# Graph message passing with residual layer norm: picking 336 instead of 294 source tiles on TensorE

## The chip, the cores and the metric

The kernel runs on one core of one Trainium2 chip. The metric is the device time of one launch in microseconds (us): the median of several runs. Next to it stands one profiled execution, from which all durations and waits are read.

A core has five engines that matter here. TensorE multiplies matrices (in the profile PE for the products and PEld for loading the stationary operand). VectorE (DVE) and ScalarE (ACT) do elementwise work. GpSimd (POOL) issues the indirect DMAs, and SyncE (SP) issues the plain ones. Each engine works through its own list of instructions in order and waits where a semaphore says so.

## The reference, cut to what matters

There are 6250 nodes with 64 features and 200000 edges, sorted by destination. Cut to its core:

```
w    = silu(edge_attr_32 @ W1 + b1) @ W2 + b2          # 200000 x 9
msg  = einsum('ef,em,fmg->eg', x[src], edge_attr_9 * w, W_tp)
agg  = segment_sum(msg, dst, 6250) / sqrt(16)
gamma, beta = split(silu(node_vec[:, None] @ Wn1 + bn1) @ Wn2 + bn2)
out  = layernorm(x + agg * (1 + gamma) + beta)
```

The costly item for this change is `x[src]`: one row of 64 floats has to be fetched for each of 200000 edges.

## The kernel before

**Tiles and groups.** Edges are cut into 1563 tiles of 128 and the tiles into 98 groups of 16 (`NBLK`, `KB`; the last group has 11). The array `hs` of a group is filled with the source rows of its 16 tiles. It has seven buffers (`AHEAD + 1`), so gathers can be up to six groups ahead.

**Three ways to fetch rows.** (1) `gather(g)`, line 91: one indirect DMA by GpSimd for each tile. (2) `load_rows`, line 106: in 16 of the groups (`SPG`, every sixth from group 7) the first tile comes as 128 single-row DMAs that SyncE issues, 22 of them in each of the six loops before. (3) `pick(g, t)`, line 482: the last `Q` = 3 tiles of each group are fetched by TensorE from a copy of x that lies in SBUF. For this the source number is split in `setup` (lines 207 to 230) into a partition, a block h of 7 and a place of 7. The first two become keys, which are written to the DRAM array `kd` and come back with `load_keys`. `keys(g, j)` multiplies the key rows with ones, so that they stand on every partition of the PSUM tile `pk` (line 458), and compares them with the partition number into the one-hot matrix `hot_k` (line 464, one VectorE instruction for three tiles). `pick` then makes 14 products of 128x128 by 128x448 (7 blocks, the two halves of x in `xs`) into the PSUM tile `px`. VectorE masks the place with `scalar_tensor_tensor` (`xm`, line 491) and sums into the column of `hs` (line 493). `px` and `xm` have two buffers each.

**The loop.** The order of all engines' work is written out by hand (`tc.manual_schedule()`). Loop i, of 98, issues in this order:

- on GpSimd `gather(i+6)`; on SyncE, in even loops, `load(i+2)` (edge features `ea` and `sh` of two groups, lines 374 and 376), in odd ones `load_keys`, then the rows of `load_rows`
- `pick(i+1, 0)`; between its products TensorE makes those of `place(i-2)` (line 559, PSUM tile `pd`) and of `keys(i+2, i-2)`, which holds the product for the gate too (line 357, into the fourth quarter of `pk`)
- `hidden(i+2)` (line 405) with its silu on ScalarE (line 413), `second(i+1)` (line 422), which writes the PSUM tile `p2`
- `windows(i)` (line 511): 32 small products of `hs` of group i; it waits for the gathers of that group, and it frees the group's buffer of `hs`
- `pick(i+1, 1)`; between its products `weights(i+1)` (the transposes of line 432, which read ScalarE's `p2s`) and `project(i-1)` (line 537, PSUM tile `pr`)
- every fourth loop, from loop 6, `finish` (lines 622 to 639): the layer norm of two blocks of nodes on VectorE and ScalarE, and the output DMA on SyncE
- `pick(i+1, 2)`

**Shared PSUM banks.** A tag of the PSUM pool is one place that is handed on in order. `pk` and `pr` share tag "r"; `pd` and `p2` share tag "s"; `px` has two places. A writer waits until the previous tile's last reader is done.

Of the kernel before, what the change touches and what calls it, by code (L numbers as in the profile page):

```python
# [7 lines left out]
F32 = mybir.dt.float32  # L8
I32 = mybir.dt.int32
BF16 = mybir.dt.bfloat16  # L10
# [5 lines left out]
P = 128  # L16
N, F, M, D, H, E = 6250, 64, 9, 32, 64, 200000
NJ = 49
# [7 lines left out]
FB = 2  # L26
AHEAD = 6
LB = 2
Q = 3
J = 7  # L30
SPG = range(7, NBLK, 6)
SPR = 22
# [16 lines left out]

def picked(g):  # L50

    return Q


def tiles(g):
# [4 lines left out]
def gnn_resnorm_kernel(ctx: ExitStack, tc: tile.TileContext, x, src, dst, dst_row, ea, sh, cn,  # L60
# [18 lines left out]
    with ExitStack() as fast:  # L79
# [56 lines left out]
        def setup(temp):  # L136
# [84 lines left out]
            nc.vector.tensor_scalar(kh, ti[1], float(P), None, op0=ALU.mult)  # L221
            for c0 in range(0, C, P):
                n = min(P, C - c0)
                p_kt = psum.tile([P, 2, P], F32, tag=("s", "r", "s")[c0 // P], name=f"p_kt{c0}")
                for i, half in enumerate((kp, kh)):
                    nc.tensor.matmul(p_kt[0:n, i, :], half[:, c0:c0 + n], ident, start=True, stop=True)
                kt = temp.tile([P, 2, P], BF16, name=f"kt{c0}")
                nc.scalar.copy(kt[0:n], p_kt[0:n])
                nc.sync.dma_start(kd[:, c0:c0 + n, :].rearrange("i c e -> c i e"), kt[0:n])
            nc.vector.scalar_tensor_tensor(jl, kh, -float(J) / P, rest, op0=ALU.mult, op1=ALU.add)  # L230
# [35 lines left out]
            def between(h):  # L266

                if h == 0:
                    p_f = psum.tile([KB, NBLK], F32, tag="s", name="p_f")
                    nc.tensor.matmul(p_f, first_t, ident[0:NBLK, 0:NBLK], start=True, stop=True)  # L270
                    nc.scalar.copy(first_f, p_f)
                elif h == 1:
                    for f in keys(0, -1):
                        f()
                elif h == 3:
                    p_cn = psum.tile([P, NJ], F32, tag="s", name="p_cn")
                    nc.tensor.matmul(p_cn, cn_j, ident[0:NJ, 0:NJ], start=True, stop=True)
                    cn_s = temp.tile([P, NJ], F32)
                    nc.scalar.copy(cn_s, p_cn)
                    nc.sync.dma_start(cn_d, cn_s)  # L280
                    nc.sync.dma_start(wn1c, wn1.rearrange("o h -> h o"))
                    nc.sync.dma_start(bn1c, bn1.unsqueeze(1))
                    gate_load(0)
                    nc.sync.dma_start(wn2a[0:H, :], wn2)
                    nc.sync.dma_start(wn2a[H:H + 1, :], bn2.unsqueeze(0))
                    for q in range(2):
                        n = (M + 1 - q) // 2
                        nc.sync.dma_start(wtc2[q * F:(q + 1) * F, 0:n, :], wtp[:, q:M:2, :])
                    load(LB)
                    with nc.allow_non_contiguous_dma(reason="2048 words, once"):  # L290
                        nc.sync.dma_start(src_r, src[:, SPG[0] * KB:NBLK * KB:6 * KB].rearrange("p g -> g p"))
# [9 lines left out]
                    hidden_act(0)  # L301
                between(h)
            pick(0, 0)
            for f in keys(1, -1):
                f()
            base(0)
            near(0)
            second(0)
# [8 lines left out]
            ids()  # L317
            hidden(1)
            nc.scalar.copy(acc_r, zero.to_broadcast([P, NJ * F]))
            pick(0, 2)  # L320
            nc.sync.dma_start(xb, x.rearrange("(j p) f -> p j f", p=P))
            for s in range(2):
                nc.sync.dma_start(w2bd[s * H:(s + 1) * H, s, :], w2)
# [30 lines left out]
            nc.scalar.activation(ht[j0 // 4 % 2][0:H, :nj], cb.pop(j0)[:, :nj], AF.Silu, bias=bn1c, scale=wn1c)  # L354

        def gate(j, pe):
            nc.tensor.matmul(pe, ht[j // 4 % 2][:, j % 4], wn2a, start=True, stop=True)
            nc.vector.tensor_scalar(gam[:, j, :], pe[:, 0:F], 1.0, 0.25, op0=ALU.add, op1=ALU.mult)
            nc.vector.tensor_add(xb[:, j, :], xb[:, j, :], pe[:, F:2 * F])

# [87 lines left out]

        hot_k = {}

        def keys(g, j):

            pk = psum.tile([P, Q + 1, P], F32, tag="r", name=f"pk{g}")
            q = picked(g)

            def part(k):
                if k == 0:
                    nc.tensor.matmul(pk[:, 0:q, :].rearrange("p t e -> p (t e)"), ones2,  # L458
                                     kr_t.pop(g).rearrange("i t e -> i (t e)"), start=True, stop=True)
                else:  # L460
                    gate(j, pk[:, Q, :])
                if k == n - 1:
                    hot_k[g] = late.tile([P, Q, J, P], F32R, tag="hot_k", name=f"hot_k{g}")
                    nc.vector.tensor_tensor(hot_k[g][:, 0:q], pk[:, 0:q].unsqueeze(2).to_broadcast([P, q, J, P]),  # L464
                                            nk[:, None, :, None].to_broadcast([P, q, J, P]), op=ALU.is_equal)

            n = 2 if 0 <= j < NJ else 1
            return [lambda k=k: part(k) for k in range(n)]

        def pick(g, t, other=()):  # L470


            other = [f for fs in other for f in fs]
            q = picked(g) if g < NBLK else 0
            if t >= q:
                for f in other:
                    f()
                return
            px = psum.tile([P, F, J], F32, tag="px", name=f"px{g}_{t}", bufs=2)
            for h in range(J):  # L480
                for i in range(2):
                    nc.tensor.matmul(px.rearrange("p f l -> p (f l)"), hot_k[g][:, t, h, :],  # L482
                                     xs[i][:, h].rearrange("p f l -> p (f l)"),
                                     start=(h == 0 and i == 0), stop=(h == J - 1 and i == 1))
                    if i == 1 and other:
                        other.pop(0)()
            for f in other:
                f()
            xm = late.tile([P, F, J], F32, tag="xm", name=f"xm{g}_{t}")
            c = (g + 1) * Q - q + t  # L490
            nc.vector.scalar_tensor_tensor(xm, li[:, None, :].to_broadcast([P, F, J]), jl[:, c:c + 1], px,  # L491
                                           op0=ALU.is_equal, op1=ALU.mult)
            nc.vector.tensor_reduce(hs[g][:, tiles(g) - q + t, :], xm, AX.X, ALU.add)  # L493
# [54 lines left out]
        def place(g):  # L548

            if not 0 <= g < NBLK:  # L550
                return []
            kb = lo_block(g)
            js = [j for j in (0, 1) if 0 <= kb + j < NJ]
            pd = {}

            def part(j):
                if j == js[0]:
                    pd[g] = psum.tile([P, 2, F], F32, tag="s", name=f"pd{g}")
                nc.tensor.matmul(pd[g][:, j, :], hot[g][:, j * P:(j + 1) * P], r[g], start=True, stop=True)  # L559
                if j == js[-1]:  # L560
                    hot.pop(g), r.pop(g)
                    b0, b1_ = kb + js[0], kb + js[-1] + 1
                    nc.vector.tensor_add(acc[:, b0:b1_, :], acc[:, b0:b1_, :], pd[g][:, js[0]:js[-1] + 1, :])

            return [lambda j=j: part(j) for j in js]

        done = 0
        with tc.manual_schedule(), tc.tile_pool(name="temp", bufs=1) as temp:
            setup(temp)

            for i in range(NBLK):
                if i + AHEAD < NBLK:
                    gather(i + AHEAD)
                if i % LB == 0 and i + LB < NBLK:
                    if i > 0:
                        load(i + LB)
                    near(i + LB)
                if i % LB == 1 and i + 1 + LB < NBLK:
                    load_keys(i + 1 + LB)
                if i % 4 == 3 and i + 1 < NJ:  # L580
                    gate_load(i + 1)
                for g in SPG:
                    if 0 < g - i <= AHEAD:
                        load_rows(g, (AHEAD - g + i) * SPR)
                pick(i + 1, 0, [place(i - 2)] + ([keys(i + 2, i - 2)] if i + 2 < NBLK else []))
                if 3 <= i <= 5:
                    reach(i - 3)
                if i + 2 < NBLK:
                    hidden(i + 2)
                if i + 1 < NBLK:  # L590
                    second(i + 1)
                if i < NBLK - 2:
                    windows(i)
                if i % 4 == 1 and i - 1 < NJ:
                    gate_hidden(i - 1)
                if i + 1 < NBLK:
                    pick(i + 1, 1, [weights(i + 1), project(i - 1)])
                else:
                    for f in project(i - 1) + place(i - 1):
                        f()  # L600
                ready = max(lo_block(i if i == NBLK - 1 else i - 1), 0)
                while ready - done >= (FB if ready < NJ - 1 else 1):
                    finish(done, min(done + FB, ready))
                    done = min(done + FB, ready)
                pick(i + 1, 2)
                if i >= NBLK - 2:
                    windows(i)
                if i == NBLK - 2:
                    sums(i + 1)
# [204 lines left out]
```

## Time and profile before

| what | value |
|---|---|
| median of 3 runs | 1590.99 us (1590.33 to 1592.33) |
| the profiled execution, its own time | 1590.71 us |
| span of the profiled execution, first to last instruction | 1588.9 us |
| around the span | 1.8 us |
| busy: TensorE / GpSimd / VectorE / ScalarE | 89% / 75% / 62% / 30% |
| granted TensorE clock, mean | 0.961 |
| gathers by GpSimd / tiles picked | 1253 / 294 |

The busy share of an engine is that of its instructions' own time. GpSimd's 75% has to be read together with its gaps: between two gathers lie 0.3 us that the profile puts down to "issue", which means that the engine waited for nothing that the profile shows. A line of a timeline gives the start, the duration, the engine and source line, and in square brackets the idle time of the engine just before, with what ended it.

### The profile page before, as it was taken

Reading aid. Unit: us, or ns where it says so; the run is one execution under the profiler, and the core shown is the slowest. Engines: PE = TensorE matmul, PEld = TensorE weight load, DVE = VectorE, ACT = ScalarE, POOL = GpSimd, SP = SyncE. Lnnn points to the kernel's source line nnn. Section 1 sums busy time; section 2 is a strip of 40 time slices with the busy share of each in tenths; the row PEclk is TensorE's granted clock in tenths of the full one; section 3 lists DMA queues with packets and bytes.
Section 4 is the critical chain, followed back from the end, with each engine's and each line's share of the span. In section 5 each row is a group of like instructions: output and inputs, shape, how many; then the busy total and the mean of one; then the engine's idle time right before and its main releaser. Section 6 shows DMA issues by size and latency. Waiting matters only on the chain.

```text
span 1588.9 us, 33055 instructions
## 1 busy us (share of the span) xinstructions
PE 1407.5 (89%) x10206; PEld 1143.1 (72%) x10206; DVE 992.6 (62%) x1611; ACT 473.1 (30%) x1187; POOL 1186.0 (75%) x1262
## 2 busy tenths in 40 slices
PE   5999999988989888989898989888889899888886
PEld 3777778767777777777676767676777777776765
DVE  6676667665656565665665656656566666565664
ACT  4323223323232323232322323323223232322232
POOL 7777777777777777777777777777777777777773
PEclk9999999999999999999999999999999999999998
DMA  5312222221211121212111221121111211211110
GB/s 155 84 48 50 62 50 54 58 50 50 61 50 50 45 66 45 50 50 61 48 47 45 52 57 47 47 62 46 45 47 47 62 46 47 62 47 45 47 46 20
DMA packets 86199, 85.42 MB, mean 54 GB/s; under 512 B 37625, under 2 KB 52013, under 8 KB 86014
## 3 DMA queue, kind: packets, MB, share of 16 engines
q0 software_dynamic: 40096, 41.14, 11.7%
q1 hardware_dynamic: 45156, 40.44, 8.4%
q8 instruction: 83, 1.36, 0.4%
q10 hardware_dynamic: 762, 1.64, 0.3%
q14 instruction: 102, 0.84, 0.2%
HBM read 81.35 MB, written 1.78 MB: 52 GB/s over the span
## 4 chain that ended last, share of the span: by engine, by line
PE 33%; POOL 32%; issue 14%; DMA 10%; SPq 7%; DVE 2%; ACT 1%; POOLq 0%; ACTq 0%; DVEq 0%
POOL hs L91 32%; PE px L482 21%; DMA hs<-in_x_dram,src_i 9%; SPq L106 4%; PE pz L511 4%; PE pr L537 2%; PE p L405 2%; SPq L101 2%; PE p L422 1%; PE p L432 1%; PE pd L559 1%; DMA ea<-in_ea_dram 1%; DVE xm L491 0%; DVE hs L493 0%; PE pk L458 0%
## 5 line engine op out<-in xcount | busy, mean ns | idle before, releaser
L91 POOL DMA_INDIRECT hs<-in_x_dram,src_i x1253 | 1184.7, 945 | 382.6 <-issue 347.3
L482 PE MATMUL px<-xs,hot_k 128*128 128x448 f32 x4116 | 1100.4, 400 | 3.2 <-DVE xs L299 3.2
L482 PEld LDWEIGHTS px<-xs,hot_k 128*128 128x128 f32 x4116 | 717.9, 196 | 62.1 <-DVE xs L299 3.6
L491 DVE SCALAR_TENSOR_TENSOR xm<-li,jl,px 128x448 f32<-128x448 f32 x294 | 199.1, 677 | 213.0 <-PE px L482 211.2
L464 DVE TENSOR_TENSOR hot_k<-pk,nk 128x2688 fp32r<-128x2688 f32 x98 | 289.4, 2953 | 4.6 <-PE pk L458 4.6
L413 ACT ACTIVATE st<-p,b1c 128x1024 f32<-128x1024 f32 x98 | 109.1, 1114 | 560.1 <-PE p L405 559.9
L511 PE MATMUL pz<-a,hs 128*64 128x72 f32 x3126 | 135.0, 245 | 134.0 <-DMA hs<-in_x_dram,src_i 79.7
L521 ACT COPY zt<-pz 64x160 f32<-64x160 f32 (+2 forms) x784 | 213.4, 272 | 128.9 <-PE pz L511 110.8
L511 PEld LDWEIGHTS pz<-a,hs 128*64 128x64 f32 x3126 | 121.1, 151 | 177.5 <-issue 161.6
L438 DVE TENSOR_TENSOR p<-p,sh 128x72 f32<-128x72 f32 x196 | 47.3, 241 | 296.0 <-PE p L432 224.3
L537 PEld LDWEIGHTS pr<-wtc,zt 128*128 128x128 f32 x980 | 190.0, 196 | 20.8 <-ACT zt L521 5.2
L493 DVE TENSOR_REDUCE hs<-xm 128x64 f32<-128x448 f32 x294 | 182.3, 620 | 10.1
L537 PE MATMUL pr<-wtc,zt 128*128 128x64 f32 x980 | 165.0, 252 | 5.0 <-ACT zt L521 5.0
L444 DVE TENSOR_TENSOR a<-oh,p 128x1152 f32<-128x1152 f32 x98 | 132.6, 1354 | 3.3
L405 PE MATMUL p<-ea,w1bd 64*128 64x512 f32 x392 | 113.5, 657 | 5.6 <-DMA ea<-in_ea_dram 5.5
L542 ACT COPY r<-pr 128x64 f32<-128x64 f32 x98 | 20.8, 212 | 261.3 <-PE pr L537 261.3
L559 PEld LDWEIGHTS pd<-r,c 128*128 128x128 f32 x388 | 73.1, 190 | 7.3 <-ACT r L542 1.0
L422 PEld LDWEIGHTS p<-st,w2p 128*32 128x32 f32 x784 | 15.6, 109 | 74.3 <-issue 72.1
L559 PE MATMUL pd<-r,c 128*128 128x64 f32 x388 | 64.6, 249 | 0.7 <-ACT r L542 0.7
L422 PE MATMUL p<-st,w2p 128*32 128x256 f32 x784 | 63.5, 396 | 0.0
L432 PE MATMUL p<-ident,p2s 128*128 128x128 f32 x196 | 58.9, 301 | 3.9 <-ACT p2s L425 3.8
L413 ACT ACT_TABLE_LOAD x23 | 29.5, 1283 | 94.7 <-PE p L405 94.7
(103 smaller groups left out, 456.6 us busy)
## 6 DMA issues: line engine op xcount, KB each, us to landing
hs<-in_x_dram SPq DMA_DIRECT2D x2048, 0.2 KB
ea<-in_ea_dram SPq DMA_DIRECT2D x49, 512.0 KB
hs<-in_x_dram,src_i POOLq DMA_INDIRECT x1253
sh<-in_sh_dram SPq DMA_DIRECT2D x49, 144.0 KB
cb<-cn_d SPq DMA_DIRECT2D x12, 128.0 KB
out_dram<-o SPq DMA_DIRECT2D x24, 64.0 KB
gam<-in_x_dram ACTq DMA_DIRECT2D x2, 448.0 KB
dst_i<-in_dst_dram SPq DMA_DIRECT2D x1, 784.0 KB
```

Source lines behind the costliest of these rows:

```text
L91: hs_dma[g] = [nc.gpsimd.indirect_dma_start(out=hs[g][:, t - g * KB, :], out_offset=None, in_=x, in_offset=bass.IndirectOffsetOnAxis(ap=sr ...
L405: nc.tensor.matmul(p1[:, i, :], w1bd[i * 64:(i + 1) * 64, :], e[i * 64:(i + 1) * 64, :], start=True, stop=True)
L413: nc.scalar.activation(st[g], p1_t.pop(g), AF.Silu, bias=b1c)
L444: nc.vector.tensor_mul(a[g], oh_t.pop(g)[:, :, None, :].to_broadcast([P, KB, M, W]), sw.unsqueeze(3).to_broadcast([P, KB, M, W]))
L464: nc.vector.tensor_tensor(hot_k[g][:, 0:q], pk[:, 0:q].unsqueeze(2).to_broadcast([P, q, J, P]), nk[:, None, :, None].to_broadcast([P, q, J ...
L482: nc.tensor.matmul(px.rearrange("p f l -> p (f l)"), hot_k[g][:, t, h, :], xs[i][:, h].rearrange("p f l -> p (f l)"), start=(h == 0 and i ...
L491: nc.vector.scalar_tensor_tensor(xm, li[:, None, :].to_broadcast([P, F, J]), jl[:, c:c + 1], px, op0=ALU.is_equal, op1=ALU.mult)
L493: nc.vector.tensor_reduce(hs[g][:, tiles(g) - q + t, :], xm, AX.X, ALU.add)
L511: mm = nc.tensor.matmul(pz[v * F:(v + 1) * F, k // 2].rearrange("p m w -> p (m w)"), hsg[:, k0 + k, :], ag[:, k0 + k].rearrange("p m w -> ...
L521: nc.scalar.copy(z[h * F:(h + 1) * F, 0:5 - h, k0 + v:k0 + n:2, :].rearrange("p m k w -> p k m w"), pz[v * F:(v + 1) * F, 0:(n + 1 - v) // ...
L537: nc.tensor.matmul(pr[g], z[:, c].rearrange("p k w -> p (k w)"), wtc2[:, c, :], start=(c == 0), stop=(c == 4))
L559: nc.tensor.matmul(pd[g][:, j, :], hot[g][:, j * P:(j + 1) * P], r[g], start=True, stop=True)
```

## The change

`Q` becomes 4, and `picked(g)` returns 4 for groups whose number is 1, 3 or 5 modulo 7, and 3 for the others: 336 tiles are picked, 42 more, and 42 fewer are gathered. Two groups of four are never neighbours. The PSUM tile `pk` of 512 floats[...] holds up to four tiles of keys. The gate's product, which had the fourth quarter of it, moves to the second half of the `pd` tile and is issued as the first product of `place`, ahead of the two that it had followed. Its two VectorE instructions follow the addition to `acc`. The one-hots are made by one VectorE instruction for each tile, into seven buffers of one tile; two of them are issued inside `pick(i+1, 0)` and the rest behind its `xm` and sum. In `setup` the arrays of keys have 392 columns instead of 294, with four chunks through PSUM instead of three.

```diff
-Q = 3
+Q = 4
...
 def picked(g):
-    return Q
+    return Q - (4 * g % 7 < 4)
...
-                p_kt = psum.tile([P, 2, P], F32, tag=("s", "r", "s")[c0 // P], name=f"p_kt{c0}")
+                p_kt = psum.tile([P, 2, P], F32, tag=("s", "r")[c0 // P % 2], name=f"p_kt{c0}")
...
-                kt = temp.tile([P, 2, P], BF16, name=f"kt{c0}")
+                kt = acc_r[:, 6 * C + c0:6 * C + c0 + P].bitcast(BF16).rearrange("p (i e) -> p i e", i=2)
...
-            pick(0, 2)
+            for t in range(2, Q):
+                pick(0, t)
...
         def gate(j, pe):
-            nc.tensor.matmul(pe, ht[j // 4 % 2][:, j % 4], wn2a, start=True, stop=True)
...
+        pk_t = {}
+        def keys(g):
+            pk_t[g] = psum.tile([P, Q, P], F32, tag="r", name=f"pk{g}")
+            nc.tensor.matmul(pk_t[g][:, 0:picked(g), :].rearrange("p t e -> p (t e)"), ones2,
+                             kr_t.pop(g).rearrange("i t e -> i (t e)"), start=True, stop=True)
+        def hots(g, t0, t1):
+            for t in range(t0, min(t1, picked(g))):
+                hot_k[g, t] = late.tile([P, J, P], F32R, tag="hot_k", name=f"hot_k{g}_{t}", bufs=7)
+                nc.vector.tensor_tensor(hot_k[g, t], pk_t[g][:, t, None, :].to_broadcast([P, J, P]),
+                                        nk.unsqueeze(2).to_broadcast([P, J, P]), op=ALU.is_equal)
...
         def place(g):
-            pd = {}
+            pd = psum.tile([P, 4, F], F32, tag="s", name=f"pd{g}")
+            pe = pd[:, 2:4, :].rearrange("p a f -> p (a f)")
...
+                    if g < NJ:
+                        gate(g, pe)
+            parts = [lambda j=j: part(j) for j in js]
+            if g < NJ:
+                parts.insert(0, lambda: nc.tensor.matmul(pe, ht[g // 4 % 2][:, g % 4], wn2a, start=True, stop=True))
+            return parts
...
-                pick(i + 1, 0, [place(i - 2)] + ([keys(i + 2, i - 2)] if i + 2 < NBLK else []))
+                pick(i + 1, 0, [place(i - 2)] + ([[lambda: keys(i + 2), lambda: hots(i + 2, 0, 2)]]
+                                                 if i + 2 < NBLK else []))
+                if i + 2 < NBLK:
+                    hots(i + 2, 2, Q)
...
-                pick(i + 1, 2)
+                for t in range(2, Q):
+                    pick(i + 1, t)
```

More of the change, by code (lines that the diff above doesn't have):

```diff
@@ L272, in between @@
                 elif h == 1:
-                    for f in keys(0, -1):
-                        f()
+                    keys(0)
+                    hots(0, 0, Q)
                 elif h == 3:
@@ L303, in setup @@
             pick(0, 0)
-            for f in keys(1, -1):
-                f()
+            keys(1)
+            hots(1, 0, Q)
             base(0)
@@ L449, in gnn_resnorm_kernel @@
         hot_k = {}
[L451 to L468, printed above, removed]
+        pk_t = {}
[8 more added lines that the diff above has]
+                                        nk.unsqueeze(2).to_broadcast([P, J, P]), op=ALU.is_equal)
         def pick(g, t, other=()):
@@ L481, in pick @@
                 for i in range(2):
-                    nc.tensor.matmul(px.rearrange("p f l -> p (f l)"), hot_k[g][:, t, h, :],
+                    nc.tensor.matmul(px.rearrange("p f l -> p (f l)"), hot_k[g, t][:, h, :],
                                      xs[i][:, h].rearrange("p f l -> p (f l)"),
@@ L553, in place @@
             js = [j for j in (0, 1) if 0 <= kb + j < NJ]
-            pd = {}
+            pd = psum.tile([P, 4, F], F32, tag="s", name=f"pd{g}")
+            pe = pd[:, 2:4, :].rearrange("p a f -> p (a f)")
             def part(j):
-                if j == js[0]:
-                    pd[g] = psum.tile([P, 2, F], F32, tag="s", name=f"pd{g}")
-                nc.tensor.matmul(pd[g][:, j, :], hot[g][:, j * P:(j + 1) * P], r[g], start=True, stop=True)
+                nc.tensor.matmul(pd[:, j, :], hot[g][:, j * P:(j + 1) * P], r[g], start=True, stop=True)
                 if j == js[-1]:
@@ L562, in part @@
                     b0, b1_ = kb + js[0], kb + js[-1] + 1
-                    nc.vector.tensor_add(acc[:, b0:b1_, :], acc[:, b0:b1_, :], pd[g][:, js[0]:js[-1] + 1, :])
-            return [lambda j=j: part(j) for j in js]
+                    nc.vector.tensor_add(acc[:, b0:b1_, :], acc[:, b0:b1_, :], pd[:, js[0]:js[-1] + 1, :])
+                    if g < NJ:
[4 more added lines that the diff above has]
+            return parts
         done = 0
```

## The prediction

> **What bounds the kernel now.** I read the page first, then the waits of TensorE, the table of windows, and TensorE's timeline at two places.
>
> ```profile
> span 1588.9 us, 33055 instructions
> PE 1407.5 (89%) x10206; PEld 1143.1 (72%) x10206; DVE 992.6 (62%) x1611; ACT 473.1 (30%) x1187; POOL 1186.0 (75%) x1262
> ...
> L91 POOL DMA_INDIRECT hs<-in_x_dram,src_i x1253 | 1184.7, 945 | 382.6 <-issue 347.3
> L482 PE MATMUL px<-xs,hot_k 128*128 128x448 f32 x4116 | 1100.4, 400 | 3.2 <-DVE xs L299 3.2
> ...
> L491 DVE SCALAR_TENSOR_TENSOR xm<-li,jl,px 128x448 f32<-128x448 f32 x294 | 199.1, 677 | 213.0 <-PE px L482 211.2
> L464 DVE TENSOR_TENSOR hot_k<-pk,nk 128x2688 fp32r<-128x2688 f32 x98 | 289.4, 2953 | 4.6 <-PE pk L458 4.6
> ```
>
> POOL's 1184.7 busy and 382.6 idle us are its whole list: 1253 gathers, one each 1.249 us, from 2.8 to 1568.3 us, next to no true wait. POOL is full at "75%". TensorE's waits:
>
> ```profile
> PE pz L511 <- DMA hs<-in_x_dram,src_i: 79.7, 39, 3.5
> PE pz L511 <- issue: 42.2, 25, 2.9
> PE pz L511 <- DMA hs<-in_x_dram: 12.0, 8, 1.8
> ```
>
> Nearly all of TensorE's recorded idle time, 133.9 us, lies ahead of `windows`, which needs the group's gathers. The windows say since when:
>
> ```profile
> 200.00:300.00 100.00, 97.17 (x739) 79.10 (x738) 70.55 (x120) 33.65 (x85) 75.61 (x81) 1.00 0.20 52
> 1000.00:1100.00 100.00, 89.04 (x652) 72.64 (x648) 60.50 (x96) 30.65 (x79) 75.60 (x81) 0.95 0.19 49
> ```
>
> Until 310 us TensorE runs without waiting for rows (97%), then at POOL's pace (89%). The first stretch shows what a loop costs TensorE alone; the second, the wait:
>
> ```profile
> 238.71 1.22 PE L511 MATMUL pz<-a,hs 128*64 128x72 f32 x32
> ...
> 244.06 3.54 PE L482 MATMUL px<-xs,hot_k 128*128 128x448 f32 x16
> 247.45 0.33 PE L559 MATMUL pd<-r,c 128*128 128x64 f32 x2
> ...
> 252.46 0.35 PE L511 MATMUL pz<-a,hs 128*64 128x72 f32 x4
> ```
>
> ```profile
> 823.04 1.22 PE L511 MATMUL pz<-a,hs 128*64 128x72 f32 x32 [2.61 <-DMA hs<-in_x_dram,src_i]
> ```
>
> TensorE needs 13.75 us (252.46 - 238.71) for a loop; POOL 13 x 1.249 = 16.24 us, or 14.99 in the 16 groups with a tile from SyncE. A pick is 14 products at 3.39/16 us (from the two middle lines): 2.95 us.
>
> **What the Trainium skill says.** "VectorE: DVE Perf Modes", The TRN2 errata, gives fp32 tensor_tensor (N+151)/0.96 ns. For N = 2688 that is 2957; the trace has 2953. So I use it for the one-hots of one tile, which no row shows: N = 896, 1091 ns (an estimate). "Perfetto Trace Analysis", DMA Instruction — SWDGE (GPSIMD): the end in the profile is that of writing descriptors, not of the data. The trace agrees: in the bound stretch `windows` starts about 2.6 us after its last gather starts, though that lasts 0.94. "TensorE: Matmul & The Clock Gate", What's actually happening: an idle window of about 3.4 us halves the clock. Here 2.75 us did: the 32 products at 839.38, after that wait, took 2.19 us instead of 1.22. With fewer waits such slow stretches go too.
>
> **The change part by part.** T is a loop's time from the first product of `pick(i+1, 0)`; in the loop above T = 0 is 247.03 (247.45 less two products).
>
> *POOL.* 42 gathers go: 42 x 1.249 = 52.5 us. The last would start at 1568.3 - 52.5 = 1515.8, and, were POOL the bound, the span would be 1536.4.
>
> *TensorE.* 42 x 2.95 = 123.9 us more. The gate's product only moves. Its loop without any wait, from the first `windows` (51.0 us) to the last (1572.1): 97 x 13.75 = 1333.8; less 46 x 0.25 = 11.5 for the loops from 51 on, which have no gate product; plus 5.9 once in loop 4, where `reach` stalls it (19.6 us against 13.75); less 1.8 in loop 0 (11.95) and 0.8 in the last two together (20.67 + 5.52). Sum 1325.6. It took 1521.1, so 195.5 us are waits and the slow clock after them. After: 1325.6 + 123.9 = 1449.5, plus the stalls that remain:
> - after each `finish` (23 of them) the silu's table load delays `p2s`, and the transposes wait: 0.76 us over their usual distance (at 154.59, 211.48, 268.62): 23 x 0.76 = 17.5
> - `hidden` waits for `ea` now and then (0.59 us at 165.72, 1.33 at 223.33). SyncE has 22 rows, 13 us, in each loop, and its output DMA waits for `finish`. With loops of 15 us on average instead of 13.75 it catches up; I keep 7 of the 24 x 0.7 us
> - `pr` waiting for bank "r", below: 3
>
> So 27.5, and the loops take 1477.0 us, 44.1 less.
>
> *Does POOL stay ahead?* Group 0's last gather starts 32.8 us before its `windows`. Per group POOL now needs 1211 x 1.249 / 98 = 15.43 us, TensorE 1477.0 / 97 = 15.23. The lead hardly shrinks, and at the end TensorE arrives at 52.3 + 1477.0 = 1529.3, POOL's rows at 1515.8 + 2.6 = 1518.4. TensorE becomes the bound, with 11 us between them.
>
> *VectorE.* 42 more `xm` and sums (0.68 + 0.62), and 336 one-hots of 1.09 for 98 of 2.95: 54.6 + 77.5 us, to 71% busy. What counts is the place. In a loop with four keys and a gate: `pk` at T + 2.36 (before 1.70), done 2.70; two one-hots, about 1.01 apart, to 4.7; `xm` and sum to 6.1; two more to 8.15. `project` wants bank "r" at T + 8.1 (255.15). Before, the one-hots were done at T + 5.8. So a reserve of 2.3 us goes in these 42 loops, almost exactly; I take 3 us over all, and bound it by 0 and 15. With three keys 1 us is left.
>
> *At nothing:* `place` and `second` share bank "s": the gate's VectorE instructions end near T + 2.6 and `second` wants it at T + 4.9; if late by more, `second` waits. Seven one-hot buffers hold 3 + 4: the one written anew belonged to a pick that ended a loop before. The fourth pick needs the `px` of the second, read while the third runs. The wider key product costs 0.05 us x 42.
>
> *Setup.* Its VectorE steps on 392 columns cost 0.1 us each more, and ahead of ScalarE's copies of x, which pace the start, comes a fourth copy (0.37) that waits for its bank: +1.3 us (0 to 3). The larger key DMAs lie on SyncE beside this.
>
> *Sum.* -44.1 + 1.3 = -42.8 us on the span: 1546.1. The execution's own time was span + 1.8 and 0.3 below the median, so **1548 us**.
>
> **The rivals.**
> 1. *POOL remains the bound*, if the stalls left are under 16: 1536.4 + 1.8 = 1538. For it: its margin is only 11 us. Against: the transposes' wait alone is 17.5.
> 2. *Waits that the gathers hid stay as in the first 310 us.* Loops 5 to 16 lost 5.1 us, 0.42 each, or 39 over 92 loops instead of my 17.5 + 7: 1562. With bank "r" at its upper bound, 12 more, 1574. For it: the stalls are in the trace; against: longer loops help SyncE.
> 3. *Slower: VectorE becomes the bound through bank "r".* Place: `pr` behind the last one-hot. The sum leaves no reserve, so what each one-hot costs beyond 1.01 us counts four times in 42 loops. It decides from 1.27 us each: 4 x 0.26 x 42 = 43.7 us, the whole gain. At 1.4 it is 4 x 0.39 x 42 = 65.5, and 3 x 0.39 - 1 in each of 55 three-key loops, 9 more: 1622. For it: a semaphore for each tile, and `place` now brings three VectorE instructions ahead of them. Against: the formula fits the present row within 0.2%.
> 4. *Nothing moves:* the extra picks' 123.9 us would have to be missing from the waits. They aren't: 195.5.
>
> **How the numbers follow.** TensorE bound with 20 to 40 us of stalls, 1541 to 1562: 0.60. POOL bound, to 1541: 0.13. More stalls, 1562 to 1588: 0.16. Within 0.2% (3.2 us, about what a measurement of this kernel can tell from no change): 0.03. Slower: 0.08. Faster is 0.89. The range begins at POOL's bound, 1538, and goes to 1573, which leaves out a third of the third case and the last two.
>
> **What would show it right or wrong.** Right: POOL's last gather starts near 1516; waits of `windows` for gathers fall from 134 to under 20 us; loops of 13.75 and 16.7 us to the end; `xm` 336 times. Wrong: waits of L534 (`pr`) for VectorE in loops with four keys, in place of those for gathers (rival 3); waits of `windows` for gathers as long as now (rival 1, or picks not issued); one-hots far from 1.09 us; a lower clock in the dense stretch, of which 1.00 at 97% busy is the sign against.

## The result, and the profile after

| | before | after |
|---|---|---|
| median | 1591.62 us (1590.33 to 1592.33, 4 runs) | 1542.95 us (1542.26 to 1543.41, 4 runs) |
| ratio after / before, 95% interval | | 0.9695 [0.9678, 0.9712] |
| span of the profiled execution | 1588.9 us | 1541.2 us |
| granted TensorE clock, mean | 0.961 | 0.984 |

The kernel is 48.7 us (3.05%) faster. The forecast was 1548 us, with a range of 1538 to 1573. One thing has to be known about the numbers further below: the kernel before takes 1591 us here and on the chip of one experiment, but 2373 to 2393 us on the three chips on which the eleven others ran, so each experiment is compared with the kernel before on its own chip only.

The page after, with the rows that answer to those shown of before:

```profile
span 1541.2 us, 34614 instructions
PE 1482.0 (96%) x10798; PEld 1217.8 (79%) x10798; DVE 1106.5 (72%) x1933; ACT 467.0 (30%) x1188; POOL 1147.7 (74%) x1220
...
PE 89%; issue 2%; ACT 2%; POOL 2%; DMA 2%; SPq 1%; DVE 1%; ACTq 0%; POOLq 0%; DVEq 0%
...
L91 POOL DMA_INDIRECT hs<-in_x_dram,src_i x1211 | 1146.4, 947 | 369.8 <-issue 332.6
L479 PE MATMUL px<-xs,hot_k 128*128 128x448 f32 x4704 | 1190.5, 388 | 4.9 <-DVE xs L299 4.2
...
L488 DVE SCALAR_TENSOR_TENSOR xm<-li,jl,px 128x448 f32<-128x448 f32 x336 | 227.7, 678 | 252.8 <-PE px L479 252.7
L464 DVE TENSOR_TENSOR hot_k<-pk,nk 128x896 fp32r<-128x896 f32 x336 | 352.2, 1084 | 10.6 <-PE pk L457 7.5
```

The row of shares that begins with "PE 89%" is the chain that ended last, by engine. The same row of the page before is:

```profile
PE 33%; POOL 32%; issue 14%; DMA 10%; SPq 7%; DVE 2%; ACT 1%; POOLq 0%; ACTq 0%; DVEq 0%
```

There two engines hand the end to each other; now one engine carries most of the chain. GpSimd's busy share is nearly what it was (74% for 75%), and its busy and idle time, 1146.4 + 369.8 us, again make up its whole list: 1211 gathers from 2.8 to 1517.2 us. The busy shares alone would not tell that its role has changed. TensorE's waits (engine, tile and line, what it waited for: us in total, times, longest) tell it:

```profile
PE p L433 <- ACT p2s L426: 11.8, 20, 0.6
...
PE pz L508 <- DMA hs<-in_x_dram,src_i: 5.2, 3, 2.8
...
PE pz L508 <- DMA hs<-in_x_dram: 1.5, 1, 1.5
...
PE pz L508 <- issue: 1.4, 1, 1.4
```

`windows` (L508, before L511) waited 133.9 us in 72 places; now it is 5.2 + 1.5 + 1.4 = 8.1 us in 5. Those that the profile puts down to "issue" are counted as waits for rows too, since these starts of `windows` also lie 2.4 to 3.3 us behind the start of the group's last gather. The largest wait of the loops is now that of the transposes (L433) for ScalarE. The two windows of before, after:

```profile
200.00:300.00 100.00, 98.82 (x715) 81.63 (x713) 75.08 (x136) 29.34 (x74) 75.66 (x80) 1.00 0.23 59
1000.00:1100.00 100.00, 98.82 (x716) 81.39 (x714) 72.54 (x124) 28.68 (x74) 75.62 (x81) 1.00 0.19 50
```

The first column after the comma is TensorE's busy time in 100 us, the third from the right its clock. The second stretch, which had 89.04 us and clock 0.95 now has 98.82 us and clock 1.00, the same as the first. The rows come late only near the end. TensorE's timeline from 1290 us on, cut to `windows` in three consecutive loops and the `px` products between:

```profile
1294.76 1.22 PE L508 MATMUL pz<-a,hs 128*64 128x72 f32 x32
...
1300.14 3.46 PE L479 MATMUL px<-xs,hot_k 128*128 128x448 f32 x16
...
1309.77 1.22 PE L508 MATMUL pz<-a,hs 128*64 128x72 f32 x32 [1.43 <-issue]
...
1326.06 2.19 PE L508 MATMUL pz<-a,hs 128*64 128x72 f32 x32 [2.79 <-DMA hs<-in_x_dram,src_i]
```

`windows` of loop 82 (the first line) finds its rows in time; those of loops 83 and 84 wait 1.43 and 2.79 us, and after the second wait the 32 products take 2.19 us instead of 1.22: the clock is halved, as after the 2.75-us wait that the prediction names. The `x16` line is read below.

### The profile page after: what moved, and what is told of

It reads as the page before. It is cut to its first block, busy times and chain, and to the rows that moved or that the text cites. A ratio compares the mean times of both kernels' runs of the same rounds, so it can differ in the third digit from the quotient of the medians.

```text
span 1541.2 us, 34614 instructions
## 1 busy us (share of the span) xinstructions
PE 1482.0 (96%) x10798; PEld 1217.8 (79%) x10798; DVE 1106.5 (72%) x1933; ACT 467.0 (30%) x1188; POOL 1147.7 (74%) x1220
## 3 DMA queue, kind: packets, MB, share of 16 engines
HBM read 80.02 MB, written 1.83 MB: 53 GB/s over the span
## 4 chain that ended last, share of the span: by engine, by line
PE 89%; issue 2%; ACT 2%; POOL 2%; DMA 2%; SPq 1%; DVE 1%; ACTq 0%; POOLq 0%; DVEq 0%
PE px L479 61%; PE pz L508 6%; PE p L406 6%; PE pr L534 5%; PE p L423 3%; PE pd L555 2%; POOL hs L91 2%; PE p L433 2%; PE pk L457 1%; SPq L106 1%; DMA hs<-in_x_dram,src_i 1%; PE pd L565 1%; ACT p2s L426 1%; ACT st L414 0%; DMA ea<-in_ea_dram 0%
## 5 line engine op out<-in xcount | busy, mean ns | idle before, releaser
L91 POOL DMA_INDIRECT hs<-in_x_dram,src_i x1211 | 1146.4, 947 | 369.8 <-issue 332.6
L479 PE MATMUL px<-xs,hot_k 128*128 128x448 f32 x4704 | 1190.5, 388 | 4.9 <-DVE xs L299 4.2
L479 PEld LDWEIGHTS px<-xs,hot_k 128*128 128x128 f32 x4704 | 815.2, 191 | 62.2 <-DVE xs L299 5.0
L488 DVE SCALAR_TENSOR_TENSOR xm<-li,jl,px 128x448 f32<-128x448 f32 x336 | 227.7, 678 | 252.8 <-PE px L479 252.7
L464 DVE TENSOR_TENSOR hot_k<-pk,nk 128x896 fp32r<-128x896 f32 x336 | 352.2, 1084 | 10.6 <-PE pk L457 7.5
L490 DVE TENSOR_REDUCE hs<-xm 128x64 f32<-128x448 f32 x336 | 208.3, 620 | 11.6
L534 PEld LDWEIGHTS pr<-wtc,zt 128*128 128x128 f32 x980 | 184.5, 191 | 22.9 <-ACT zt L518 4.7
L508 PEld LDWEIGHTS pz<-a,hs 128*64 128x64 f32 x3126 | 107.6, 139 | 48.8 <-issue 45.4
L508 PE MATMUL pz<-a,hs 128*64 128x72 f32 x3126 | 122.1, 232 | 8.2 <-DMA hs<-in_x_dram,src_i 5.2
L433 PE MATMUL p<-ident,p2s 128*128 128x128 f32 x196 | 54.6, 279 | 11.8 <-ACT p2s L426 11.8
```

Source lines behind the costliest of these rows:

```text
L91: hs_dma[g] = [nc.gpsimd.indirect_dma_start(out=hs[g][:, t - g * KB, :], out_offset=None, in_=x, in_offset=bass.IndirectOffsetOnAxis(ap=sr ...
L464: nc.vector.tensor_tensor(hot_k[g, t], pk_t[g][:, t, None, :].to_broadcast([P, J, P]), nk.unsqueeze(2).to_broadcast([P, J, P]), op=ALU.is_ ...
L479: nc.tensor.matmul(px.rearrange("p f l -> p (f l)"), hot_k[g, t][:, h, :], xs[i][:, h].rearrange("p f l -> p (f l)"), start=(h == 0 and i ...
L508: mm = nc.tensor.matmul(pz[v * F:(v + 1) * F, k // 2].rearrange("p m w -> p (m w)"), hsg[:, k0 + k, :], ag[:, k0 + k].rearrange("p m w -> ...
L534: nc.tensor.matmul(pr[g], z[:, c].rearrange("p k w -> p (k w)"), wtc2[:, c, :], start=(c == 0), stop=(c == 4))
```

## The experiments

Two theories stood against each other. **A:** GpSimd's list of gathers set the pace; each tile that is picked instead of gathered takes 1.25 us off it, until TensorE's list, which grows with each pick, is as long. **B:** the rearrangement itself (the one-hots tile by tile, the gate's product in front of `place`) brings part of the gain. All edits are made to the kernel after.

**Sixteen gathers more, and no rows by SyncE.** `load_rows` is left out; GpSimd gathers those tiles too, 1227 in all.

```
-  for t in range(g * KB + (g in SPG), g * KB + tiles(g) - picked(g))]
+  for t in range(g * KB, g * KB + tiles(g) - picked(g))]
...
-  for g in SPG:
-      if 0 < g - i <= AHEAD:
-          load_rows(g, (AHEAD - g + i) * SPR)
```

> The changed kernel with all unpicked tiles gathered by GpSimd: the 2048 single-row DMAs of SyncE are gone, and GpSimd has 1227 gathers instead of 1211. Theory A (GpSimd's list at 1.25 us for each gather, level with TensorE's in the changed kernel): GpSimd is the bound again and every gather counts: 16 x 1.25 = 20 us more, 1562 us where the kernel before takes 1591, and TensorE waits some 30 us for rows. If TensorE alone is the bound: 1543 us. On the chips of the eight runs so far, where the kernel before took 2390 us: if SyncE's long list of rows is what holds the engines up there (loops were 24 us with rows and 13.5 us in the last six loops, which have almost none), the time falls to some 1600 us; if not, it stays above 2300.

Measured: 1562.64 us, beside 1591.16 for the kernel before on that chip, one run of each. The page of this kernel, then the first of TensorE's waits, then the same window as above:

```profile
span 1560.8 us, 27959 instructions
PE 1485.6 (95%) x10798; PEld 1220.4 (78%) x10798; DVE 1106.3 (71%) x1933; ACT 467.1 (30%) x1188; POOL 1163.1 (75%) x1236
...
PE 78%; POOL 9%; issue 5%; DMA 4%; ACT 2%; DVE 2%; SPq 0%; ACTq 0%; POOLq 0%; DVEq 0%
```

```profile
PE pz L508 <- DMA hs<-in_x_dram,src_i: 25.4, 15, 5.0
PE p L433 <- ACT p2s L426: 11.5, 20, 0.6
```

```profile
1000.00:1100.00 100.00, 94.39 (x676) 78.56 (x675) 68.00 (x117) 28.58 (x73) 75.61 (x81) 0.97 0.23 56
```

TensorE's work is the same to 4 us (1485.6 against 1482.0), its transposes wait as long, and a loop of three picks takes 13.45 us without a gate product in both. What differs is GpSimd: its last gather starts at 1537.4 instead of 1517.2, 20.2 us later for 16 gathers, 1.26 us each, and the span is 19.6 us longer. The waits of `windows` are back. So at 336 picks the kernel stands just where the two lists are level: 16 gathers more and GpSimd sets the end again, at its full price. The row of shares alone would not tell: TensorE still has 78% of the chain that ended last, for `windows` waits only from loop 60 on. The run also shows that the rows by SyncE, 13 us of its queue in a loop, do not slow TensorE here: without them its loop is not shorter. What SyncE's rows do on the slower chips, about which the expectation asks too, this chip could not show; the next runs do.

**The rearrangement without the extra picks**, three times, on three chips: `picked` returns 3, so the 294 tiles and 1253 gathers of before, with everything else of the change.

```
-    return Q - (4 * g % 7 < 4)
+    return 3
```

> The changed kernel with three picks in every group (294), so that only its rearrangement is left: one-hots tile by tile, the gate's product in front of placing, the longer setup. Theory A (two lists: GpSimd at 1.25 us for each gather, TensorE at 2.75 us for each pick, and the time is that of the later one; the rearrangement brings nothing): 1253 gathers as before, 1591 to 1595 us, waits of windows for gathers 110 to 140 us. Theory B (the rearrangement itself brings the gain, through VectorE's order or the shorter distance of products, 0.200 instead of 0.207 us): 1545 to 1570 us. The distance of px products tells too whether it comes with the tile-by-tile one-hots (0.200) or with the fourth tile (0.207).

> The kernel of e1_three once more (three picks in every group, the rearrangement alone), since in the first series TensorE's products had gaps of about 1 us put down to issue and the kernel before took 2390 us there. Theory A (two lists, GpSimd at 1.25 us for each gather, TensorE at 2.75 us for each pick; the time is that of the later one): as the kernel before, ratio 1.000 to 1.003, waits of windows for gathers 110 to 140 us. Theory B (the rearrangement brings the gain): ratio 0.97 to 0.99.

> Three picks in every group (294), the rearrangement alone, as e1 and e5. On a chip where the kernel before takes 1591 us: theory A (two lists, GpSimd at 1.25 us for each gather, TensorE at 2.75 us for each pick; the time is that of the later one) expects 1591 to 1595 us and 110 to 140 us of waits of windows for gathers; theory B (the rearrangement brings the gain) 1545 to 1570 us.

Measured, over the kernel before on the same chip: 2406.53 / 2389.64 = 1.0073 [1.0056, 1.0089]; 2410.17 / 2392.89 = 1.0071 [1.0044, 1.0099]; 2381.82 / 2372.58 = 1.0044 [1.0032, 1.0055]. No gain; theory B falls for these chips. Theory A's numbers are missed as well: the ratio lies above 1.003, and `windows` hardly waits for gathers (5.2 us in the last of the three, and no more than 6.1 in the others), so these runs test A no further. For the chip of the result there is no run with 294 picks; its trace says that the rearrangement made TensorE's work no shorter: three-pick loops with a gate product take 13.79 us in the kernel after and took 13.75 before.

What these chips do differently can be read from the last of the three. Its windows while gathers run, and after the last gather (2279.4 us):

```profile
1000.00:1100.00 100.00, 68.19 (x433) 52.65 (x435) 44.00 (x83) 20.67 (x50) 49.50 (x53) 0.80 0.15 34
2295.00:2335.00 40.00, 38.40 (x299) 31.27 (x298) 27.75 (x46) 12.55 (x34) 0.00 (x0) 1.00 0.11 35
```

And a loop of each stretch on TensorE's timeline:

```profile
1208.15 0.68 PE L406 MATMUL p<-ea,w1bd 64*128 64x512 f32 x1 [0.35 <-issue]
1210.23 1.92 PE L406 MATMUL p<-ea,w1bd 64*128 64x512 f32 x2 [1.40 <-issue]
...
1215.78 1.08 PE L423 MATMUL p<-st,w2p 128*32 128x256 f32 x8 [2.41 <-DVE xb L360]
...
2310.85 1.13 PE L406 MATMUL p<-ea,w1bd 64*128 64x512 f32 x4
2311.91 0.64 PE L423 MATMUL p<-st,w2p 128*32 128x256 f32 x8
```

With gathers running, the four products of `hidden` are torn apart by "issue" and `second` waits for VectorE; without them (GpSimd 0.00 busy) the same products take 1.13 us without a gap and TensorE is 96% busy (38.40 of 40) at full clock. Loops 10 to 87 take 23.5 us on average, the five after the last gather 13.45 to 14.92, as on the other chips. SyncE's rows are not the cause: 127 of them are still issued behind the last gather, 0.41 us apart in the median, in just these five loops and the one behind them. (The expectation of the first experiment took these loops to have almost no rows; they have as many as the others.) The waits of GpSimd:

```profile
POOL hs L91 <- PE pz L508: 729.8, 90, 32.6
POOL hs L91 <- issue: 348.8, 1111, 9.8
```

A gather itself is no slower (0.944 us, and 1.25 apart when it may start), but GpSimd waits 729.8 us for `windows` to free a buffer of `hs`. So on these chips GpSimd's list is not the bound: it is ahead by all the buffers there are, and the loops of TensorE, stretched while gathers run, set the pace.

**More or fewer picks, on those chips.** 322 (groups 1 and 5 of each seven have four) and 343 (every odd group has four).

```
-    return Q - (4 * g % 7 < 4)
+    return Q - (g % 7 not in (1, 5))     # 322
+    return Q - (g % 2 == 0)              # 343
```

> The changed kernel with four picks in two groups of seven (1 and 5), 322 in all. Theory A: GpSimd has 1225 gathers and stays the bound from about the middle on; 14 gathers more than with 336 are 17.5 us: 1561 us, and some 60 to 70 us of waits of TensorE. Theory B: TensorE has 14 picks less to do, the rearrangement stays: 1540 us or below.

> The changed kernel with four picks in every odd group, 343 in all, seven more. Theory A: GpSimd has 1204 gathers and is no bound anywhere; TensorE has 7 x 2.75 = 19 us more and loses its last 12 us of waits for rows: 1551 us, no wait of windows for gathers. If GpSimd alone set the time (the picks hidden): 1543 - 9 = 1534 us. If bank r and VectorE bound it (theory C): 49 loops with four keys instead of 42, above 1555 us with waits of pr for VectorE.

> The kernel of e3_343 once more (four picks in every odd group). Theory A: GpSimd is no bound anywhere, TensorE has 19 us more and loses 12 of waits: 1551 us, ratio 0.974. If GpSimd alone set the time: 1534 us. Theory C (bank r and VectorE): above 1555 us with waits of pr for VectorE.

> Four picks in every odd group, 343 in all, as e3 and e7. Where the kernel before takes 1591 us: theory A expects TensorE as the bound, 7 x 2.75 = 19 us more less 12 of waits for rows: 1551 us; if GpSimd alone set the time: 1534 us; theory C (bank r and VectorE): above 1555 us with waits of pr for VectorE.

Measured: 322 gives 2460.95 / 2389.64 = 1.031 [1.0289, 1.0332]. 343 gives 2523.97 / 2389.64 = 1.056 [1.0543, 1.0578], 2524.11 / 2392.89 = 1.0533 [1.0489, 1.0576] and, on the third chip, 2470.9 / 2372.58 = 1.0405 [1.0374, 1.0436]. The numbers expected were for a chip like that of the result and are missed altogether: where TensorE's loops set the pace, each pick that is added costs, and the gather that it saves gives back less. The optimum of picks on a chip like that of the result was not measured: no run with 322 or 343 fell on one.

**Lighter GpSimd at 336 picks.** In every even group without a row load one gather less, 1162 in all. The kernel leaves out these tiles' rows, and `windows` multiplies those of the second tile in their place.

```
-  for t in range(g * KB + (g in SPG), ...
+  for t in range(g * KB + (g in SPG or g % 2 == 0), ...
...
-  hsg[:, k0 + k, :], ...
+  hsg[:, max(k0 + k, int(g not in SPG and g % 2 == 0)), :], ...
```

> The changed kernel with 49 further gathers left out (the first tile of the even groups that don't get it from SyncE; windows multiplies the second tile's rows in its place, so the first tile's messages are wrong), all 336 picks as they are: TensorE's own floor. Theory A with both lists equal in the changed kernel: only the 9 to 12 us of waits for rows in loops 82 to 94 go, 1531 us; windows waits for no gather. If GpSimd were still the bound through the whole kernel: 49 x 1.25 = 61 us less, 1482 us. If gathers don't matter any more: 1543 us.

Measured: 2430.41 / 2392.89 = 1.0156 [1.0128, 1.0185]. It was meant to show TensorE's own floor on a chip like the first; there it was not measured. Here it gives a price. From 294 picks and 1253 gathers (2410 us) to 336 and 1162 is +20 us; from there to 343 and 1204 (2524) is +94. If each pick costs p and each gather q, 42p - 91q = 20 and 7p + 42q = 94: p = 3.9 and q = 1.6 us (an estimate from these three runs). A tile that changes sides then costs 2.3 us net; for the 28 of the 322 version that is 65 us over the 294 version, where 54 were measured. So by this estimate the change of this case, 42 tiles, would be some 4 to 5% slower on such a chip, between the 3.1% and the 5.3 to 5.6% of 28 and 49 tiles on the chips of these runs. It was not run there.

**The one-hots in one instruction again**, at 343 picks, three or four tiles at once, one buffer for each size.

```
+  hk = late.tile([P, q, J, P], F32R, tag=f"hot_k{q}", name=f"hot_k{g}", bufs=1)
+  nc.vector.tensor_tensor(hk, pk_t[g][:, 0:q]..., nk[:, None, :, None]..., op=ALU.is_equal)
```

> As e3 (343 picks), but the one-hots of a group in one VectorE instruction for three or four tiles, issued where the first two were; two buffers, of three and of four tiles. Theory A: TensorE is the bound and has no wait for VectorE, so the time is that of e3 within 3 us, or a little longer if the xm behind a one-hot of 3.9 us comes late. Theory C (splitting them is what keeps bank r and px in time): slower than e3 by 10 us or more, with waits of px or pr for VectorE. The distance of px products says whether the one-hot's buffers set it: 0.207 us with one buffer for several tiles, 0.200 if not.

Measured: 2529.23 / 2389.64 = 1.0605 [1.056, 1.0649], against 1.056 [1.0543, 1.0578] for tile by tile on the same chip. The intervals overlap; on a chip where TensorE waits for VectorE for other reasons this says little about bank "r" on the chip of the result.

**The silu's table loaded ahead.** At 343 picks, a silu of one element behind `finish`, so that the table load does not fall into the next `hidden`.

```
+  nc.scalar.activation(silu_o, eps[0:1, :], AF.Silu)
```

> e7 with one instruction more in finish: ScalarE makes a silu of one element behind the square root, so that the silu's table is loaded there and not between hidden and the transposes. Theory A (TensorE is the bound in e7, so its 22 waits of 0.75 us count in full): 22 x 0.75 = 16.5 us less than e7, less what comes back as waits for rows: 1535 to 1539 us, a version below the changed kernel. If TensorE isn't the bound in e7: no difference to e7.

> e11 and a silu of one element behind the square root of finish, as e8. Where the kernel before takes 1591 us: if TensorE is the bound in e11, its 22 waits of 0.75 us for the table load count, less what comes back as waits for rows: 1535 to 1539 us, below the changed kernel's 1543. If not: as e11.

Measured: 2523.1 / 2392.89 = 1.0543 [1.0513, 1.0572] and 2471.26 / 2372.58 = 1.0406 [1.0376, 1.0436], against 1.0533 and 1.0405 without the silu on the same chips: no difference. The load did move: the transposes' waits for ScalarE, 13.0 and 9.5 us in the two kernels without the silu, are gone. On these chips, then, waits of TensorE can go without any gain. Whether it gains where TensorE is dense stays open.

## Why the prediction was right, point by point

**GpSimd (right).** 52.5 us less and a last gather at 1515.8 were forecast; it starts at 1517.2, and one gather is 1.249 us after the other in the median. The sixteen gathers put back confirm the price.

**TensorE becomes the bound (right up to loop 82, wrong in the margin).** The sum gave the loops 1477.0 us; measured from the first `windows` (55.28) to the last (1524.25) they are 1469.0. By terms:

- *A pick, 2.95 us:* a loop with a fourth pick is 2.74 to 2.85 us longer (13.79 to 16.53 with a gate product, 13.45 to 16.30 without), so 42 x 0.15 = 6 us too much. The prediction's quotient, 14 x 3.39/16, is 2.97, and the first of its 16 distances is a longer one, 0.29 us; the others are 0.207 us, and 14 of those are 2.90. The rest is a shorter distance: where `px` products follow one another they now start 0.200 us apart (14 x 0.200 = 2.80), and the `x16` line above has 3.46 us, that of before 3.54. The distance is 0.200 with three picks as well, and with the one-hots made in one instruction, so neither the fourth tile nor the division of the one-hots is its cause; where the buffers lie wasn't tried.
- *Transposes after `finish`, 17.5:* the 20 waits in the lines shown of the result cost 0.82 us each (0.76 ahead of the first transpose, 0.06 between the two), 16.4.
- *`hidden` waiting for `ea`, 7:* one wait of 0.7 us. That the longer loops gave SyncE more relief than was allowed for fits its waits for the output of `finish`, which fell from 172.9 to 119.7 us, and is not shown further.
- *Bank "r", 3:* less than 0.1 us in any loop. Two one-hots take 2.08 us together; the estimate from the Trainium skill's formula ("VectorE: DVE Perf Modes", The TRN2 errata), 1091 ns for one, stands against 1084 measured, so rival 3 had no ground: it needed 1.27 us. VectorE's busy time grew by 113.9 us, not 132: the one-hots take 62.8 us more instead of 77.5, since two in a row overlap.
- *`reach` in loop 4, 5.9:* 4.7.
- *Rows, 0:* this term was missing. In loops 83, 84, 91, 93 and 95 `windows` starts 8.5 us later in all than it usually does after `second`, and the slow clock after one of these waits costs 2.7: 11 us.

That is -6 -1 -6 -3 -1 +11 = -6 us, where -8 was measured; 2 us are not assigned.

**The step that failed: "the lead hardly shrinks".** The lead is the time from the start of a group's last gather to its `windows`. Three of these gathers on GpSimd's timeline, of groups 0, 82 and 83, whose `windows` start at 55.27, 1294.76 and 1309.77 us:

```profile
18.69 0.94 POOL L91 DMA_INDIRECT hs<-in_x_dram,src_i  x1 [0.30 <-issue]
1290.98 0.94 POOL L91 DMA_INDIRECT hs<-in_x_dram,src_i  x1 [0.30 <-issue]
1307.21 0.94 POOL L91 DMA_INDIRECT hs<-in_x_dram,src_i  x1 [0.30 <-issue]
```

The lead falls from 36.6 us to 3.8 in loop 82 and 2.6 in loop 83, where `windows` waits. The prediction compared 15.43 us per group on GpSimd with 15.23 on TensorE, and even that difference, 0.2 x 97 = 19 us, is over half of the lead. Moreover, 15.43 was a mean over 98 groups, with the last one short (7 gathers); the 97 others need 1204 / 97 x 1.2515 (the mean distance of two gathers) = 15.53. TensorE took (1294.76 - 55.28) / 82 = 15.12. So 0.4 us go in each loop, 33 in 82 loops. The prediction looked at the end alone, where it saw 11 us of margin. There the lead is 7.0 us again, since loop 95 takes 22.5 us, so 4.4 us of margin are left; but the lead had been used up from loop 83 on, and the waits of loops 83 to 95 come from that. The forecast was near by luck in this part: TensorE's loops were over-priced by more than the late rows cost. The two lists are level: with the 16 gathers more, GpSimd leads again.

**Setup, +1.3 within 0 to 3 (too low).** The first `windows` starts 4.3 us later (55.28 for 50.96). The mechanism of the prediction is there, at a higher price: ScalarE's copies of x begin 2.2 us later (15.79 for 13.63), behind VectorE's longer steps and the fourth copy of keys, and the last `px` product of the first pick starts 2.15 us later. The other 2.1 us are a term that was missing: TensorE's products then run slower. Four products and a pick of 14, before and after:

```profile
28.81 1.58 PE L247 MATMUL p_b<-xb,ones 1*128 1x392 f32 x4
31.33 4.23 PE L482 MATMUL px<-xs,hot_k 128*128 128x448 f32 x14
```

```profile
31.01 2.44 PE L247 MATMUL p_b<-xb,ones 1*128 1x392 f32 x4
34.39 4.95 PE L479 MATMUL px<-xs,hot_k 128*128 128x448 f32 x14
```

From 31 to 51 us the granted clock is 0.66 here; it was 0.84 to 0.85. Why it is lower is not shown; TensorE's wait ahead of the first `px` product is longer (4.03 us for 2.99). The four one-hots of group 1 take 4.07 us for 2.95 and hold nothing up: VectorE waits for TensorE behind them (1.83 us).

**Sum.** 1546.1 - 8.0 + 3.0 = 1541.1 us of span, measured 1541.2. The measured median, 1542.95, lies halfway between the forecast and rival 1 (GpSimd bound, 1538): GpSimd's list and its 24.0 us behind the last gather start set the end as much as TensorE does. Rival 2 fell with the waits for `ea`; rival 4 with the 133.9 us of waits, of which 8.1 are left.

## What to carry to other kernels

When work is moved from the engine that bounds to one that waits for it, compare the two lists per unit of the loop, over the full units only, and follow the lead of one over the other to the end: a few tenths of a microsecond in a loop use up a lead of 30 us in 80 loops. Look at every loop, not at the last alone, where a long loop can hide that the lead was gone before. The gain ends where the lists are level, and it is made only where the engine relieved is really the bound: on three chips where GpSimd waited for TensorE, 28 or 49 moved tiles cost 3 to 6%. A step of a sum that comes out near can hide two wrong terms of opposite sign; the trace of the changed kernel shows which.

## What the runs showed of the hardware that was not expected

- The same program has two paces on different chips: the kernel before takes 1591 us in the measurement of the result and on the chip of one experiment, and 2373 to 2393 on three. In the slower case single gathers are unchanged (0.944 us), but while they run, the four products of `hidden` are torn apart by "issue", VectorE is late, and SyncE's row DMAs start 1.27 us apart on average; while GpSimd pauses it is 0.68 (both of the last run with three picks; in the kernel after it is 0.65). As soon as the last gather is done the loops take what they take elsewhere. That the gathers and the feeding of the other engines compete there is suggested by this, and not shown: no run took the gathers away.
- `px` products with the same shapes and operand types that follow one another start 0.207 us apart in one kernel and 0.200 in another, at full clock. That holds for some 14 of the 42 `px` products of a three-pick loop, and the loop is not shorter for it (13.79 for 13.75 us). The cause is open.
- The length of a wait does not decide whether TensorE's clock is halved. Two waits of the kernel before:

```profile
726.66 2.19 PE L511 MATMUL pz<-a,hs 128*64 128x72 f32 x32 [2.10 <-issue]
1144.15 1.22 PE L511 MATMUL pz<-a,hs 128*64 128x72 f32 x32 [2.72 <-DMA hs<-in_x_dram,src_i]
```

  After 2.10 us the 32 products run at half clock, after 2.72 us at full clock. The clock records of both traces change only at whole multiples of 3.413 us from one another, which suggests that it also counts when a wait falls; no run tested it. The Trainium skill ("TensorE: Matmul & The Clock Gate", What's actually happening) gives an idle window of about 3.4 us for the halving; here waits of 2.1 to 2.9 us were enough, and the measurement decides.
